# Cross-attention in one core: keys and values by seven block products in place of eight, with a new order of VectorE's work

## The chip, the cores and the metric

The kernel runs on one core of a Trainium2 chip. A core has TensorE (PE in the profile: matrix products, with PEld for the loads of their stationary operand), VectorE (DVE), ScalarE (ACT), GpSimd (POOL) and SyncE (SP, which issues DMAs). Each engine works through its own queue of instructions in order; semaphores tie them together. The products land in PSUM, eight banks of 512 float32 columns on 128 partitions. The metric is the device time of one execution in microseconds (us), lower is better; where several runs are compared it is their median.

## The reference, cut to what matters

All arrays are float32: `x` is 16 x 100 x 640, the context 16 x 722 x 384. The first 718 rows of the context (`enc`) give keys and values; the last 4 (`ca`) go through a second, small attention.

```python
enc, ca = ctx[:, :718], ctx[:, 718:]
hs = mha(x @ Wq, enc @ Wk, enc @ Wv)              # 8 heads of 80, softmax over 718 keys
q1 = einsum('btc,th->bch', ca, Wq_ca)[:, picked]  # 100 of the 384 rows
hs1 = mha(q1, x, x)                               # softmax over 100 keys
hs2 = mha(hs1 @ Wq, ca @ Wk_ca, ca @ Wv_ca)       # softmax over 4 keys
out = (hs + hs2) @ Wout + b_out + x
```

## The kernel before, in words

The 16 batches are worked through one after the other by a Python loop that is unrolled into one program (L743 to L864). In each batch `b`:

- **Scores.** `scores` (L342) multiplies keys by queries for two chunks of key rows at a time. `KC` cuts the 718 rows into five chunks of 128 and one of 78. The result lies in a PSUM tile of four banks (`psum4`, one such tile), from which ACT copies it to `st` (L369), 800 columns (8 heads x 100 queries) for each chunk.
- **Values.** `values` (L247) makes V for a chunk: two halves of 320 columns, each from three products (384 input features are three blocks of 128). The last 78 rows of four batches are taken together: `load_tails` loads them, `last_values` (L278) multiplies them in transposed form once in four batches, and `values` turns them back by transposes (L254). ACT or DVE copies V out of PSUM (L269).
- **Maximum.** DVE takes the maximum of `st` over chunks into `top` (L775, L784, L792), then `over_partitions` (L387) carries it over the partitions: a transpose (L390), a reduction (L392), four copies `side` (L395), four reductions `mx` (L398), a spreading copy (L405), a transpose back (L407). Then it is subtracted from each chunk (L808) and ACT takes the exponential (L810).
- **The second attention** is class `Second`. `products` (L433) makes `y` on PE, `scores1` (L462) makes `e1` on GpSimd, `softmax1` runs the same maximum over `e1` on DVE, `softmax2` (L488) multiplies it by `y` (`z`, L493), takes the softmax over four keys and issues the DMA of `vb` on GpSimd's queue; `values2` (L535) sums on GpSimd. `values2` waits for the last subtraction of L808, and `scores1` and `keys` of later batches follow it in GpSimd's queue.
- **The output.** Class `Last` transposes the result of the batch before (L588), copies it to `hsT` (L597), and `project` (L602) multiplies by `Wout` whenever 128 rows are complete: in all batches but 0, 1, 5, 10 and 14 for the batch before, and DVE adds `x` and bias (L620).
- **Keys of the next batch.** `keys1` (L322): five blocks of 128 columns, two halves of 359 rows, three products each (L329), copied by ACT to `kT` (L336), with the exponentials placed between these copies.
- **Queries** of the next two batches, every second batch (L302).
- **The weighted sum** `a_ps` (L845): 192 products of `st` and V; DVE divides by the sums of the exponentials and adds `hs2` (L853 to L861).

PSUM tiles other than the scores' come from a pool of four single banks (`psum1`): a new tile waits until a bank's last reader is done.

The order on an engine is a planner's, except for GpSimd, which keeps the program's order inside the loop (`manual_schedule`, L742). `issue_after` puts an instruction behind a named one of its own engine. All products are float32, and each shows as two records in the trace.

Of the kernel before, what the change touches and what calls it, by code (L numbers as in the profile page):

```python
# [10 lines left out]
ALU = mybir.AluOpType  # L11
# [10 lines left out]
KC = [(k, min(P, SK - k)) for k in range(0, SK, P)]  # L22
LK, LT = KC[-1]
# [51 lines left out]
VH = [(0, 0, 0, P, 0), (0, 1, 0, P, P), (1, 3, 0, P, 64), (1, 4, 0, P, 192)]  # L75
VH += [(0, 2, 0, 64, 2 * P), (1, 2, 64, P, 0)]
KH = SK // 2
# [3 lines left out]
def kernel(  # L81
# [28 lines left out]
    ps4 = ctx.enter_context(tc.tile_pool(name="ps4", bufs=1, space=PSUM))  # L110
    ps1 = ctx.enter_context(tc.tile_pool(name="ps1", bufs=4, space=PSUM))

    def psum4(name):
        return ps4.tile([P, RG, 512], F32, tag="ps4", name=name)
# [8 lines left out]
    def scores_tile(name):  # L123
        return main.tile([P, ROWS], F32, tag="st", name=name, bufs=len(KC) + 1)
# [21 lines left out]
    def enc_tile(name):  # L146
        return inp.tile([P, CC, SK], F32, tag="enc", name=name)

    def load_enc(b):
        enc = enc_tile(f"enc_{b}")  # L150
        nc.sync.dma_start(out=enc, in_=enct[b])
        return enc

    def load_tails(g):
        tail = inp.tile([P, CC, 4, LT], F32, tag="tail", name=f"tail_{g}", bufs=1)
        for c in range(CC):
            in_order(
                nc.sync.dma_start(
                    out=tail[:, c],
                    in_=enct[4 * g : 4 * g + 4, :, c, LK:].rearrange("b p k -> p b k"),  # L160
                )
            )
        return tail
# [11 lines left out]
    wvca_sb = enc_tile("wvca")[:, :, :H]  # L175
    enc = enc_tile("enc_0")
    for c in range(CC):
        in_order(nc.sync.dma_start(out=enc[:, c, :P], in_=enct[0][:, c, :P]))
        for cols in [slice(0, H // 2), slice(H // 2, H)] if c == 0 else [slice(0, H)]:
            nc.scalar.dma_start(  # L180
                out=wv_sb[:, c, cols], in_=wv[c * P : (c + 1) * P, cols]
            )
    for lo, hi in [(P, 3 * P), (3 * P, SK)]:
        in_order(nc.sync.dma_start(out=enc[:, :, lo:hi], in_=enct[0][:, :, lo:hi]))
# [11 lines left out]
    wq_in = [scores_tile(f"wq_{c}")[:, :H] for c in range(HC)]  # L196
    for c in range(HC):
        in_order(nc.sync.dma_start(out=wq_in[c], in_=wq[c * P : (c + 1) * P]))
    tail = load_tails(0)
# [3 lines left out]

    vs = []
    for k, n in KC:
        v = const.tile([n, NH, D + 1], F32, name=f"v_{k}")
        nc.gpsimd.memset(v[:, :, D : D + 1], 1.0)
        vs.append(v)

# [37 lines left out]
    def values(b, i, enc, engines):  # L247

        k, n = KC[i]
        v_pss = [psum1(f"v_ps_{b}_{i}_{g}") for g in range(2)]  # L250
        if k == LK:

            for g, c, lo, hi, at in VH:
                nc.tensor.transpose(  # L254
                    v_pss[g][:n, at : at + hi - lo],
                    vt[lo:hi, c, (b % 4) * LT : (b % 4 + 1) * LT],
                    ident[lo:hi, lo:hi],
                )
        for g, (engine, v_ps) in enumerate(zip(engines, v_pss)):
            if k != LK:  # L260
                for c in range(CC):
                    nc.tensor.matmul(  # L262
                        v_ps[:n, : 4 * D],
                        enc[:, c, k : k + n],
                        wv_sb[:, c, g * 4 * D : (g + 1) * 4 * D],
                        start=(c == 0),
                        stop=(c == CC - 1),
                    )
            engine(  # L269
                vs[i][:, 4 * g : 4 * g + 4, :D],  # L270
                v_ps[:n, : 4 * D].rearrange("p (h d) -> p h d", d=D),
            )


    def vt_tile(g):
        return inp.tile([P, HC, 4 * LT], F32, tag="vt", name=f"vt_{g}", bufs=1)

    def last_values(g, vt, tail, chunks):  # L278
        for n in chunks:
            t_ps = psum1(f"vt_ps_{g}_{n}")  # L280
            for c in range(CC):
                nc.tensor.matmul(  # L282
                    t_ps[:, : 4 * LT],
                    wv_sb[:, c, n * P : (n + 1) * P],
                    tail[:, c].rearrange("p b k -> p (b k)"),
                    start=(c == 0),
                    stop=(c == CC - 1),
                )
            nc.scalar.copy(vt[:, n], t_ps[:, : 4 * LT])
# [8 lines left out]
    def queries(p, xT, tiles, n):  # L298
# [12 lines left out]
        else:  # L311

            for u in range(2):
                nc.vector.tensor_tensor(  # L314
                    qz[:, 0, :, u * S : (u + 1) * S],
                    q_ps[:, : 2 * S].rearrange("p (j s) -> p j s", j=2),
                    qmask[:, u : u + 1].unsqueeze(2).to_broadcast([P, 2, S]),
                    ALU.mult,
                )


    def keys1(b, enc, chunks, stages=()):  # L322

        stages = list(stages)
        for n in chunks:
            for g in range(2):
                k_ps = psum1(f"kT_ps_{b}_{n}_{g}")
                for c in range(CC):
                    nc.tensor.matmul(  # L329
                        k_ps[:, :KH],  # L330
                        wk_sb[:, c, n * P : (n + 1) * P],
                        enc[:, c, g * KH : (g + 1) * KH],
                        start=(c == 0),
                        stop=(c == CC - 1),
                    )
                copied = nc.scalar.copy(kT[:, n, g * KH : (g + 1) * KH], k_ps[:, :KH])  # L336
                if stages:
                    with tc.issue_after(copied.ins):
                        stages.pop(0)()


    def scores(b, g, tiles):  # L342
# [3 lines left out]
        for a in range(2):  # L346
            k, n = KC[2 * g + a]
            for c in range(HC):
                for r in range(RG):
# [4 lines left out]
                    else:  # L354
                        rhs, lo, hi = qz[rows, 0, b % 2], 0, 2 * S
                    nc.tensor.matmul(  # L356
                        s_ps[:n, r, 256 * a + lo : 256 * a + hi],
# [6 lines left out]
        es = []  # L364
        for a in range(2):
            i = 2 * g + a
            n = KC[i][1]
            e = scores_tile(f"st_{b}_{i}")[:n]
            copied = nc.scalar.copy(  # L369
                e.rearrange("p (r q) -> p r q", r=RG),  # L370
                s_ps[:n, :, 256 * a : 256 * a + 2 * S],
            )
            es.append(e)
        return es, copied
# [12 lines left out]
    def over_partitions(top, name):  # L387

        turned = wide(f"turned_{name}").rearrange("p (b k) -> p b k", k=32)
        nc.vector.transpose(turned.rearrange("p b k -> p (b k)"), top)  # L390
        quad = small.tile([P, NB], F32, tag="quad", name=f"quad_{name}")
        nc.vector.tensor_reduce(quad, turned, AX.X, ALU.max)  # L392
        side = small.tile([32, 4, NB], F32, tag="side", name=f"side_{name}")
        for j in range(4):
            nc.vector.tensor_copy(side[:, j, :], quad[32 * j : 32 * j + 32, :])  # L395
        mx = small.tile([P, NB], F32, tag="mx", name=f"mx_{name}")
        for j in range(4):
            nc.vector.tensor_reduce(  # L398
                mx[32 * j : 32 * j + 32, :],
                side.rearrange("p q b -> p b q"),  # L400
                AX.X,
                ALU.max,
            )
        spread = wide(f"spread_{name}").rearrange("p (b k) -> p b k", k=32)
        nc.vector.tensor_copy(spread, mx.unsqueeze(2).to_broadcast([P, NB, 32]))  # L405
        over = wide(f"over_{name}")
        nc.vector.transpose(over, spread.rearrange("p b k -> p (b k)"))  # L407
        return over
# [13 lines left out]
    class Second:  # L422


        def __init__(self, b, xT):
            self.b, self.xT = b, xT[:, b % 2]

# [5 lines left out]
        def products(self):  # L433
# [14 lines left out]
            nc.vector.tensor_reduce(  # L448
# [4 lines left out]
            )  # L453
            self.y = ys[b % 2]
            self.copied = nc.vector.tensor_copy(
# [24 lines left out]
        def softmax1(self):  # L480
            over = over_partitions(e1, f"1_{self.b}")
            nc.vector.tensor_tensor(e1[:S], e1[:S], over[:S], ALU.subtract)

        def exponentials1(self):
            with tc.issue_after(copied.ins):
                nc.scalar.activation(e1[:S], e1[:S], AF.Exp, scale=SCALE)

        def softmax2(self):  # L488
            b = self.b
            z_ps = psum1(f"z_ps_{b}")  # L490
            for h in range(NH):
# [14 lines left out]
            )  # L506
            s2 = small.tile([S, NH, T], F32, tag="s2", name=f"s2_{b}")
# [12 lines left out]
            nc.scalar.activation(e, e, AF.Exp, scale=SCALE)  # L520
            sm = small.tile([S, NH], F32, tag="sm2", name=f"sm2_{b}")
# [7 lines left out]
            self.vb = vb = vb_tile(f"vb_{b}")  # L529
            nc.gpsimd.dma_start(  # L530
                out=vb[:S],
                in_=va_d[b * T : (b + 1) * T, :].unsqueeze(0).to_broadcast([S, T, H]),
            )
# [27 lines left out]
    class Last:  # L561
# [19 lines left out]
        def transpose(self, chunks=[(0, HC)]):  # L581
# [4 lines left out]
            for c0, c1 in chunks:  # L586
# [4 lines left out]
                for r, (lo, n) in enumerate(OC):  # L591
# [5 lines left out]
                    nc.vector.tensor_copy(  # L597
# [39 lines left out]
    for i in range(len(KC) - 1):  # L637
        values(0, i, enc, (act, dve))
# [14 lines left out]
    room = scores_tile("k2T")  # L653
# [40 lines left out]
    second.products()  # L694
# [3 lines left out]
    with tc.issue_after(second.copied.ins):  # L698
# [13 lines left out]
    keys1(0, enc, range(HC))  # L712
# [29 lines left out]
    ctx.enter_context(tc.manual_schedule(engines={mybir.EngineType.Pool}))  # L742
# [175 lines left out]
```

## Time and profile before

| | |
|---|---|
| median of 3 runs | 1051.35 us (1048.66 to 1051.49) |
| the profiled execution's own time | 1049.26 us |
| its span in the trace | 1047.6 us, granted clock 0.998 |
| matrix records | 11119 |
| start of `a_ps`, batches 0, 7, 8, 10, 15 | 106.3, 553.1, 611.2, 731.6, 1030.6 us |
| a batch, from `a_ps` to `a_ps` | 58.05 us (even), 66.51 (odd, with queries), 74.62 (odd, with queries and tails) |
| DVE busy per batch, mean of batches 1 to 15 | 32.4 us |

The profile is that of one execution. Its page gives busy time by engine, the chain of work that ended last, and groups of instructions by source line. The timeline lists instructions in order of time, with the start and the length of each merged run. A group reads like this: line, engine, operation, what is written from what, shapes, count, busy time in all, mean of one in ns, then the idle time just before and what ended it.

### The profile page before, as it was taken

To read this page: it belongs to the slowest core of one execution; us is meant where nothing else is said; L and a number is where in the kernel's file an instruction comes from. 1 tells how busy PE (TensorE), PEld (TensorE's weight loads), DVE (VectorE), ACT (ScalarE), POOL (GpSimd) and SP (SyncE) were. 2 spreads that over 40 slices of the span, in tenths; PEclk is the share of its full clock that TensorE was granted. 3 is DMA by queue.
4 is the path that set the end of the run, shared out by engine and by line. 5 is a ranking of instruction groups with operands and counts; after the bars stand their busy time and mean duration, and the time that the engine had idled before them with its cause. 6 is when DMAs were issued, how large, how long until landed. Compare 5 with 4: busy or idle time off the path is not lost.

```text
span 1047.6 us, 24702 instructions
## 1 busy us (share of the span) xinstructions
PE 1033.3 (99%) x11119; PEld 774.5 (74%) x11119; DVE 538.6 (51%) x997; ACT 310.2 (30%) x567; POOL 418.9 (40%) x373
## 2 busy tenths in 40 slices
PE   9998999999999999999999999999999999999997
PEld 6784868777687777867778677776868768687775
DVE  1358553828238282565705648064750737528295
ACT  1224231233412334233142332333222233313331
POOL 4629035090720807236180260805445053350833
PEclk9999999999999999999999999999999999999999
DMA  8641011111121111211120211101111021110011
GB/s 280 203 169 46 32 43 47 41 55 40 69 65 34 62 41 43 67 68 47 67 59 27 70 47 63 42 30 43 48 68 46 2 64 48 65 41 1 2 40 33
DMA packets 24347, 61.82 MB, mean 59 GB/s; under 512 B 8462, under 2 KB 14614, under 8 KB 20722
## 3 DMA queue, kind: packets, MB, share of 16 engines
q1 hardware_dynamic: 20994, 42.38, 12.5%
q0 software_dynamic: 2512, 16.72, 4.9%
q8 instruction: 87, 1.43, 0.6%
q10 hardware_dynamic: 736, 1.15, 0.3%
q14 instruction: 18, 0.15, 0.0%
HBM read 55.98 MB, written 4.26 MB: 58 GB/s over the span
## 4 chain that ended last, share of the span: by engine, by line
PE 96%; DVE 3%; DMA 0%; ACT 0%; issue 0%; ACTq 0%; DVEq 0%
PE kT_ps L329 27%; PE v_ps L262 25%; PE s_ps L356 12%; PE a_ps L845 11%; PE q_ps L302 6%; PE o_ps L610 6%; PE vt_ps L282 3%; PE y_ps L439 1%; DVE st L808 1%; PE z_ps L493 1%; PE v_ps L254 1%; PE hst_ps L588 1%; PE m_ps L669 1%; DMA wv_sb<-in_wv 0%; DVE side L395 0%; DVE top L792 0%
## 5 line engine op out<-in xcount | busy, mean ns | idle before, releaser
L544 POOL TENSOR_TENSOR hs<-vb,p 100x640 f32<-100x640 f32 x64 | 84.2, 1324 | 567.9 <-DVE p L525 565.4
L329 PE MATMUL kT_ps<-enc,wk_sb 128*128 128x359 f32 x960 | 296.6, 468 | 6.3 <-ACT kT L336 4.3
L262 PE MATMUL v_ps<-wv_sb,enc 128*128 128x320 f32 x960 | 276.8, 439 | 1.7 <-DVE xn L620 1.1
L329 PEld LDWEIGHTS kT_ps<-enc,wk_sb 128*128 128x128 f32 x960 | 179.9, 190 | 115.4 <-ACT kT L336 5.4
L262 PEld LDWEIGHTS v_ps<-wv_sb,enc 128*128 128x128 f32 x960 | 177.8, 190 | 77.8 <-issue 7.2
L369 ACT COPY st<-s_ps 128x800 f32<-128x800 f32 x96 | 74.5, 828 | 237.4 <-PE s_ps L356 237.4
L269 ACT COPY v<-v_ps 128x320 f32<-128x320 f32 x126 | 53.3, 424 | 209.9 <-PE v_ps L262 202.3
L336 ACT COPY kT<-kT_ps 128x359 f32<-128x359 f32 x160 | 73.1, 458 | 140.8 <-PE kT_ps L329 140.8
L845 PEld LDWEIGHTS a_ps<-v,st 128*36 128x36 f32 (+3 forms) x3072 | 108.9, 125 | 6.5 <-issue 6.3
L845 PE MATMUL a_ps<-v,st 128*36 128x81 f32 (+3 forms) x3072 | 111.9, 233 | 0.5 <-issue 0.5
L314 DVE TENSOR_TENSOR qz<-q_ps,qmask 128x200 f32<-128x200 f32 x16 | 5.1, 361 | 192.5 <-PE q_ps L302 192.5
L356 PE MATMUL s_ps<-qp,kT 32*128 32x100 f32 (+1 forms) x3072 | 102.5, 269 | 0.0
L356 PEld LDWEIGHTS s_ps<-qp,kT 32*128 32x128 f32 (+1 forms) x3072 | 94.1, 179 | 10.2 <-issue 7.3
L469 POOL TENSOR_TENSOR e<-ca,g 100x800 f32<-100x800 f32 x64 | 98.8, 1554 | 5.4 <-DMA ca<-in_cas 2.9
L808 DVE TENSOR_TENSOR st<-st,over 128x800 f32<-128x800 f32 x96 | 100.0, 1076 | 0.4
L853 DVE RECIPROCAL rs<-a_ps 100x4 f32<-100x4 f32 x32 | 5.8, 182 | 183.2 <-PE a_ps L845 183.2
L476 POOL TENSOR_TENSOR e<-e,e 100x800 f32<-100x800 f32 x48 | 91.5, 1906 | 3.8
L810 ACT ACTIVATE st<-st 128x800 f32<-128x800 f32 x96 | 83.6, 872 | 21.3 <-DVE st L808 21.3
L551 POOL TENSOR_TENSOR hs<-hs,hs 100x640 f32<-100x640 f32 x48 | 77.1, 1606 | 3.8
L610 PE MATMUL o_ps<-wout_sb,hsT 128*128 128x320 f32 (+2 forms) x260 | 72.4, 433 | 0.0
L302 PEld LDWEIGHTS q_ps<-xT,wq_sb 128*128 128x128 f32 x400 | 67.9, 190 | 2.1 <-issue 0.5
L302 PE MATMUL q_ps<-xT,wq_sb 128*128 128x200 f32 x400 | 69.1, 333 | 0.0
(81 smaller groups left out, 873.1 us busy)
## 6 DMA issues: line engine op xcount, KB each, us to landing
enc<-in_enct SPq DMA_DIRECT2D x15, 1077.0 KB
vb<-va_d POOLq DMA_DIRECT2D x16, 1000.0 KB, 5.9
xT<-in_xt SPq DMA_DIRECT2D x8, 500.0 KB
xn<-in_x SPq DMA_DIRECT2D x11, 320.0 KB
out<-xn SPq DMA_DIRECT2D x11, 320.0 KB
ca<-in_cas SPq DMA_DIRECT2D x16, 156.2 KB
tail<-in_enct SPq DMA_DIRECT2D x12, 156.0 KB
wout_sb<-in_wqt SPq DMA_DIRECT2D x1, 1600.0 KB
```

What stands on the lines that cost most here:

```text
L262: nc.tensor.matmul(v_ps[:n, : 4 * D], enc[:, c, k : k + n], wv_sb[:, c, g * 4 * D : (g + 1) * 4 * D], start=(c == 0), stop=(c == CC - 1),)
L302: nc.tensor.matmul(q_ps[:, : 2 * S].rearrange("p (j s) -> p j s", j=2), wq_sb[:, c, n * P : (n + 1) * P], xT[:, :, c, :], start=(c == 0), ...
L329: nc.tensor.matmul(k_ps[:, :KH], wk_sb[:, c, n * P : (n + 1) * P], enc[:, c, g * KH : (g + 1) * KH], start=(c == 0), stop=(c == CC - 1),)
L356: nc.tensor.matmul(s_ps[:n, r, 256 * a + lo : 256 * a + hi], kT[rows, c, k : k + n], rhs, start=(a == 0 and c == 0), stop=(c == HC - 1), s ...
L469: first = nc.gpsimd.tensor_tensor(to, self.ca[:, t, :].unsqueeze(1).to_broadcast([S, NH, S]), g[:, :, t].unsqueeze(2).to_broadcast([S, NH, ...
L476: nc.gpsimd.tensor_tensor(e, e, to, ALU.add)
L544: first = nc.gpsimd.tensor_tensor(to, vb[:S, t, :].rearrange("p (h d) -> p h d", h=NH), p2[:, :, t].unsqueeze(2).to_broadcast([S, NH, D]), ...
L551: nc.gpsimd.tensor_tensor(sums, sums, to, ALU.add)
L610: nc.tensor.matmul(o_ps[k][:n, : H // 2], hsTs[r][:, c, :n], wout_sb[:, c, k * (H // 2) : (k + 1) * (H // 2)], start=(c == 0), stop=(c == ...
L808: less = nc.vector.tensor_tensor(st[i], st[i], over[:n], ALU.subtract)
L810: lambda e=st[i]: nc.scalar.activation(e, e, AF.Exp, scale=SCALE)
L845: nc.tensor.matmul(a_v[lo:hi, h % 4], st[i][:, h * S + lo : h * S + hi], vs[i][:, h, :], start=(i == 0), stop=(i == len(KC) - 1),)
```

## The change

The 718 rows are now two halves of 359 (`KH`), each cut into 128, 128 and 103 rows; chunk `i` of the first half and of the second form pair `i`. Two blocks of rows by two blocks of input features by two blocks of columns are multiplied with seven products instead of eight (sums S1 to S4 of `enc` and T1 to T4 of the weights are made ahead, on GpSimd); the third block of features is multiplied as before and added into the same banks, so a pair of V, or two column blocks of K, takes 11 products instead of 12. The tails and their transposes are gone. The fifth column block of K (`last_keys`) keeps six products.

A `Blocks` object does this in two steps: four products into four banks, then seven more on top of them. DVE adds three times after each step, ACT copies once.

```diff
+class Blocks:
+    def first_half(self, room=None):
+        self.banks = room or [psum1(f"{self.name}_ps_{j}") for j in range(4)]
+        c11, c12, c21, c22 = self.to
+        m = self.sum(0, ("11", "11"), first=True)
+        self.copies = [nc.scalar.copy(c22, m)]
+        m = self.sum(1, ("S2", "T2"), first=True)
+        nc.vector.tensor_tensor(c21, m, c22, ALU.add)
+        m = self.sum(2, ("S1", "T1"), first=True)
+        nc.vector.tensor_tensor(c22, m, c22, ALU.add)
+        m = self.sum(3, ("S3", "T3"), first=True)
+        nc.vector.tensor_tensor(c22, m, c22, ALU.add)
+    def second_half(self):
+        c11, c12, c21, c22 = self.to
+        m = self.sum(0, ("12", "21"), ("31", "31"), last=True)
+        self.copies.append(nc.scalar.copy(c11, m))
+        m = self.sum(2, ("S4", "22"), ("31", "32"), last=True)
+        nc.vector.tensor_tensor(c12, m, c21, ALU.add)
+        m = self.sum(3, ("22", "T4"), ("32", "31"), last=True)
+        nc.vector.tensor_tensor(c21, m, c21, ALU.add)
+        m = self.sum(1, ("32", "32"), last=True)
+        nc.vector.tensor_tensor(c22, m, c22, ALU.add)
...
-    ctx.enter_context(tc.manual_schedule(engines={mybir.EngineType.Pool}))
+    engines = {mybir.EngineType.Pool, mybir.EngineType.PE, mybir.EngineType.DVE}
+    ctx.enter_context(tc.manual_schedule(engines=engines))
```

The four-bank tile becomes four tiles of one bank, so ACT copies a pair of score chunks (`st` now holds pairs of 2 x 800 columns) by four copies of 400 columns, one for each bank. The order on PE and DVE is now the program's too. In batches 1 to 13 it is (`va`, `vb`, `vc` are the V pairs, `ka` and `kb` the key blocks; `Maximum` is `over_partitions` in five steps, `go(n)` issues n of them; `side` is now made by reductions):

```python
scores(0); most = max(st[0])          # GpSimd: enc_sums(next enc), last.load()
va.first_half()
scores(1); larger(1)                  # two maxima into most
va.second_half()
scores(2)
now.softmax1(2); last.transpose(); larger(2)
vb.first_half(); now.softmax1(2)
vc.first_half(room)                   # room: the scores' four banks
now.softmax1(); top.go(2)             # rest of e1's maximum and its subtraction
vb.second_half(); now.exponentials1(); top.go(1)
vc.second_half(); top.go()
subtract(0); last.project(); second.products()
now.softmax2(); ka.first_half(room)   # ACT: second.copy()
now.scores2(); subtract(1); now.softmax3()
kb.first_half(); less = subtract(2)
ka.second_half(); kb.second_half(); last_keys()
exponentials                          # GpSimd: values2(less), scores1, keys
queries every second batch; a_ps
```

Batch 0 makes its V by ordinary products, 36 of them, and its maximum follows both first halves of the next keys; the sums of the weights are made in it on GpSimd. In batch 14 the `y` of the last batch comes ahead of `vb`, its `scores1` ahead of `values2`, and its `softmax1` at the end. In batch 15 `softmax2` and `values2` come right after the first scores, and the projection after `vc`. Copies of `hsT` and `y` and the masked copies of `qz` move from DVE to ACT.

## Prediction

> **What bounds the kernel now.** I read the page's busy shares and chain by engine first.
>
> ```profile
> PE 1033.3 (99%) x11119; PEld 774.5 (74%) x11119; DVE 538.6 (51%) x997; ACT 310.2 (30%) x567; POOL 418.9 (40%) x373
> ...
> PE 96%; DVE 3%; DMA 0%; ACT 0%; issue 0%; ACTq 0%; DVEq 0%
> ```
>
> TensorE (PE) is never idle, and 96% of the chain is its own work, so a product less is its pitch less, as long as nothing new makes PE wait. Pitches come from PE's timeline, from a piece's start to the next one's. Batch 8 starts at 560.00 and ends at 618.04.
>
> ```profile
> 576.12 3.42 PE L262 MATMUL v_ps<-wv_sb,enc 128*128 128x320 f32 x12
> 579.38 5.55 PE L610 MATMUL o_ps<-wout_sb,hsT 128*128 128x320 f32 x20
> ...
> 592.10 0.79 PE L254 MATMUL v_ps<-ident,vt 128*78 128x128 f32 x6
> 592.81 18.41 PE L329 MATMUL kT_ps<-enc,wk_sb 128*128 128x359 f32 x60
> 611.15 6.97 PE L845 MATMUL a_ps<-v,st 128*64 128x81 f32 x192
> ```
>
> Each product is two records. A V product takes (579.38-576.12)/6 = 0.543 us (0.541 inside longer runs), a K product 18.34/30 = 0.611 (0.605 without the 0.2 of a start). Next, VectorE (DVE), on which the change puts its additions:
>
> ```profile
> 488.13 1.00 DVE L390 STREAM_TRANSPOSE turned<-e 128x800 f32<-128x800 f32 x1
> 489.17 0.99 DVE L392 TENSOR_REDUCE quad<-turned 128x25 f32<-128x800 f32 x1
> 490.19 0.71 DVE L395 COPY side<-quad 32x25 f32<-32x25 f32 x4
> 490.93 1.32 DVE L398 TENSOR_REDUCE mx<-side 32x25 f32<-32x100 f32 x4
> 492.28 0.99 DVE L405 COPY spread<-mx 128x800 f32<-128x800 f32 x1
> 493.31 1.01 DVE L407 STREAM_TRANSPOSE over<-spread 128x800 f32<-128x800 f32 x1
> 494.35 0.99 DVE L482 TENSOR_TENSOR e<-e,over 100x800 f32<-100x800 f32 x1
> ...
> 502.37 2.07 DVE L792 TENSOR_TENSOR top<-top,st 128x800 f32<-128x800 f32 x2
> ...
> 508.87 0.49 DVE L620 TENSOR_TENSOR xn<-o_ps,xn 128x320 f32<-128x320 f32 x1
> 509.27 0.97 DVE L405 COPY spread<-mx 128x800 f32<-128x800 f32 x1
> ...
> 511.33 2.79 DVE L808 TENSOR_TENSOR st<-st,over 128x800 f32<-128x800 f32 x3
> ```
>
> A maximum with its subtraction is 7.13 us; two `top` steps 2.1; a subtraction's pitch 0.93; an addition out of PSUM (L620) 0.49, pitch 0.40.
>
> **PE's work.** V: before 30 products and 0.71 of transposes a batch, and 15 products (8.33 us) for four batches' tails; after, three pairs of 11. In all, 480 x 0.541 + 60 x 0.555 + 16 x 0.71 = 304.4 against (36 + 15 x 33) x 0.541 = 287.3: -17.1. K: 480 products against 30 + 15 x 28 = 450: -18.2. Scores: 103 rows cost between the 2.67 of two full chunks and the 2.47 of 128 + 78; I take 2.57: +1.6. Together -33.7. An even batch becomes 7.91 scores, 18.31 V, 0.48 transposes, 5.38 projection, 1.06 y, 0.68 z, 17.04 K, 6.89 a_ps = 57.75, the same as batch 8's 58.04: the gain lies in the tails, of which batches 3, 7 and 11 have 8.3 us each, batch 0 8.4.
>
> **What DVE takes on.** A batch gets 30 PSUM additions (18 of 320 columns, 12 of 359); copies of V, y, hsT and qz leave it. That is about 30 x 0.41 - 1.95 - 0.41 - 0.74 - 0.32 = +8.8 on the 32.4 of now: 41 of 58 us. DVE and PE both run in written order, so what counts is the order. A clock from batch start (t = 0):
>
> PE without waits: scores of pair 2 end at 14.2; transposes 14.7; four products of vb 16.95, of vc 19.1, vb's seven 22.9, vc's 26.7; projection 32.1; y 33.15; z 33.8; ka's four 36.3. Then kb's first four need four single banks, and all are held: two by the projection, one by y, one by z, until DVE has read them.
>
> DVE begins at 16.0 (14.2 + 0.14 + four ACT copies of 400 columns: 1.55 for two of 800 bounds them below, 4 x 0.46 of the 359 copy above; I take 1.66). Then: two `most` steps 2.11; vb's additions 0.40 + 0.50 + 0.45 = 1.35 (the third reads the second's result); side, mx, spread 3.06; vc's 1.35; transpose and e subtraction 1.95; `top`'s transpose and reduction 1.99; vb's 1.27; side and mx 2.1; vc's 1.27; spread and transpose 2.06; subtraction of 1600 columns 1.77 (two pitches of 0.93 less one start of 0.09; two durations, 1.96, above): 36.3. The two projection additions end at 36.75 and 37.15, y's sum at 37.35, z at 37.85. So kb starts at 36.75 instead of 36.3: **0.45 us of waiting a batch, 58.2**. Later K steps find their additions done (kb's second at 43.65, needed at 44.7). Everything after t = 16 is one queue; a microsecond more on DVE is one more for PE.
>
> Moves that I cost at nothing: copies of hsT, y and qz go to ACT, which is busy 18 of 58 us; the exponentials (three of 1600 columns, twice 0.87 less a start) follow K's copies and the last subtraction at 46 and end at 48.4, before a_ps at 51.3. If ACT is late with hsT, vb's fourth product waits for its bank, 0.3, in the shadow of kb's wait. The tails' 12 DMAs leave SP's queue; GpSimd issues vb 5.9 us of flight and more before values2. One tile per bank adds no work to PE.
>
> The side reductions have no equal row: four copies 0.71 below, L398's 1.32 above; they resemble the copies (25 columns from 25), so 0.75. Block additions lie between 0.40 and the full 0.49.
>
> **GpSimd.** Its 23 us (values2, scores1, keys; 520.62 to 544.1 in batch 7) wait for the last subtraction, which moves from t = 32 to 46. So after an even batch they run to t = 12 of the odd one, with enc_sums (four of 359 columns; between 0.39 of 128x96 and 1.61 of 100x640, 0.87 by length) and xn to 18. What that costs DVE, batch 0 shows:
>
> ```profile
> 72.95 3.33 DVE L784 TENSOR_TENSOR top<-top,st 128x800 f32<-128x800 f32 x2 [0.85 <-ACT st L369]
> ```
>
> 3.33 instead of 2.1 for two, with GpSimd at work: 1.67 each. Two of L792 in the same batch took 3.75, four of L808 in batch 15 8.09 (2.02 each); 1.03 is the bound below, 2.02 the one above, and I take L784, the same operation. L620 stayed at 0.49 beside GpSimd, so block additions are not slowed. The two steps of pair 1 then end at 12.85 instead of 11.6, the e1 steps at 16.15, pair 2's steps at about 19: DVE is 0.9 late, and part of it is taken up. **Odd batches wait 1.1 us: 67.3** (66.2 with queries). After odd batches GpSimd is done by t = 9: nothing. [...]
>
> enc_sums waits for enc's DMA. It leaves behind the output store, t = 37 of the batch before, and 1.08 MB at the page's 200 to 280 GB/s lands by 43, 15 us early. Behind it queue xn, the vb load and values2, none due before 35.
>
> **Batches without a projection** (1, 5, 10, 14): PE has 5.38 us less, DVE only 0.85 less. kb ends at 37.7 instead of 39.2. In 10, z waits for a vb bank until 29.1, ka's second product for vc's banks until 32.4; the subtraction ends at 36.3, y's sum at 36.5, z at 37.0, and the fourth product of kb follows. So 10 becomes 56.7 (work 52.4; now 53.94); 14, with the next scores1 beside its subtractions, 57.2 (now 53.26); 1 and 5, with 60.8 of work, the 4.3 of batch 10 and 0.3 and 0.8 from GpSimd, 65.4 and 65.9 (now 61.71).
>
> **Ends.** Batch 0 waits for the exponentials. Scores end 5.6 us earlier (6 products in place of 15 and the transposes), block additions give 2.8 back, GpSimd slows the subtractions as now; a_ps starts between 99 (now 106.4) and 105.3, if the last key product waits for a bank and the exponentials behind its copy. I take 101.4: -5. Batch 15: PE 38.1 until a_ps, subtractions done at 35.7, exponentials 37.4; the 4 us of waits at 1024 to 1030 go: 46.6 becomes 45: -1.6.
>
> **Sum.** Five even batches +0.8; five odd ones 356.9 to 336.5: -20.4; 1 and 5 +7.9; 10 and 14 +6.7; ends -6.6. Total -11.6 on the profiled run's own 1049.26 (span 1047.6): 1038. The median of the runs, 1051.35, is 0.2% above that run.
>
> [...]
>
> **Rivals.**
> - *DVE is quicker.* If its queue is 5% shorter (additions overlap more), about 1 us a batch comes back: 0.45 x 5 + 1 x 9 = 11: 1026. For: every pitch here is below its duration. Against: the additions wait for three engines. No waits at all would give about 1010.
> - *DVE decides everything: slower.* Additions cost their full 0.49 because each waits for a semaphore: 12 x 0.09 ahead of kb, and 0.1 at each of six joints: 1.7 a batch, 14 x 1.7 = 24: 1062. It decides from about 1 us a batch. For: a queue with no gap from t = 16 to 48, and GpSimd's overlap could reach further. Against: L620 between other work.
> - *The gain is eaten up exactly*: 0.6 to 1.0 a batch more than worked out, 1046 to 1052. That the products are not saved at all is excluded by their count in the code, 11 for 12.
>
> **Chances.** 0.3%, about what can be told from no change, is 3.2 us: 1046.1 to 1052.4 is the same. Forecast (1031 to 1046) 0.42; quicker DVE 0.24; no change 0.14; slower 0.20. So faster 0.66, same 0.14, slower 0.20. The range goes from half-way past the first rival, 1020, to nearly the second, 1060.
>
> **What would show it.** V records 1062, K 900. Batch 8 near 58.2, 7 near 67.3, 10 near 56.7, a_ps of batch 0 at 101.4. kb's first products waiting for DVE's xn or z; DVE near 650 us busy. Wrong if PE waits elsewhere (for ACT's copies, for enc_sums), if batch 8 is over 59.5, or if contended steps exceed 2 us.

## The result, and the profile after

The changed kernel takes 1057.47 us (median of 5 runs, 1056.67 to 1060.87) where the kernel before takes 1051.35 (5 runs, 1048.66 to 1051.49): 1.0071 times as long, with a 95% interval from 1.0050 to 1.0093. It is slower by 0.7%, more than the 0.3% that can be told from no change. The profiled execution is the median itself; its span is 1055.8 us, 8.2 above that of before. The forecast of 1038 was wrong in sign; the time lies inside the range, between "eaten up exactly" and the slower rival.

The page's busy shares and its chain by engine, and three of its groups:

```profile
PE 1012.4 (96%) x10945; PEld 745.3 (71%) x10945; DVE 711.7 (67%) x1277; ACT 281.3 (27%) x567; POOL 505.1 (48%) x439
...
PE 63%; DVE 27%; issue 6%; ACT 3%; DMA 0%; DVEq 0%; ACTq 0%
...
L941 DVE TENSOR_TENSOR most<-most,st 128x800 f32<-128x800 f32 (+1 forms) x64 | 82.7, 1292 | 46.5 <-ACT st L505 45.4
...
L299 PE MATMUL k_ps<-enc,wk_sb 128*128 128x359 f32 x240 | 85.0, 476 | 10.0 <-DVE xn L787 7.3
L930 DVE TENSOR_TENSOR st<-st,over 128x1600 f32<-128x1600 f32 (+1 forms) x48 | 91.5, 1910 | 0.5
```

TensorE has 174 records fewer, just the 18 of V, 60 of K and 96 of transposes that were counted, and is busy 20.9 us less. The saving is there, but the span is longer: TensorE went from 99% to 96%, and VectorE, which held 3% of the chain, holds 27%. What TensorE waits for, by the view of waits (engine, line, what it waited for, then us in all, how many times, the longest):

```profile
PEld k_ps L299 <- DVE xn L787: 13.0, 10, 1.6
...
PE room L299 <- DVE v L329: 7.6, 4, 1.9
PE k_ps L299 <- DVE xn L787: 7.3, 10, 1.0
...
PE a_ps L1103 <- DVE kT L329: 6.3, 1, 6.3
```

These are banks: kb's first product (`k_ps`) waits for the bank that VectorE's L787 reads last, ka's second (`room`) for one of vc's additions. The third view is the timeline. TensorE in batch 8, around the place where the prediction put the wait (start, length, then in brackets the idle time before):

```profile
591.88 0.87 PE L299 MATMUL room<-enc,wk_sb 128*128 128x359 f32 x2
592.58 1.37 PE L299 MATMUL room<-enc,wk 128*128 128x359 f32 x4
593.79 0.77 PE L299 MATMUL room<-enc,wk_sb 128*128 128x359 f32 x2
595.06 0.87 PE L299 MATMUL k_ps<-enc,wk_sb 128*128 128x359 f32 x2 [0.50 <-DVE xn L787]
```

VectorE in the same batch, whose first score product starts at 558.03:

```profile
573.87 2.02 DVE L941 TENSOR_TENSOR most<-most,st 103x800 f32<-103x800 f32 x2 [0.93 <-ACT st L505]
575.81 0.48 DVE L318 TENSOR_TENSOR v<-v_ps,v 128x320 f32<-128x320 f32 x1
576.39 0.49 DVE L320 TENSOR_TENSOR v<-v_ps,v 128x320 f32<-128x320 f32 x1
576.99 0.49 DVE L322 TENSOR_TENSOR v<-v_ps,v 128x320 f32<-128x320 f32 x1
577.40 0.70 DVE L542 TENSOR_REDUCE side<-quad 32x25 f32<-32x25 f32 x4
...
585.86 0.48 DVE L329 TENSOR_TENSOR v<-v_ps,v 128x320 f32<-128x320 f32 x1
586.44 0.49 DVE L331 TENSOR_TENSOR v<-v_ps,v 128x320 f32<-128x320 f32 x1
586.85 0.48 DVE L333 TENSOR_TENSOR v<-v_ps,v 128x320 f32<-128x320 f32 x1
...
592.77 1.82 DVE L930 TENSOR_TENSOR st<-st,over 128x1600 f32<-128x1600 f32 x1
594.52 0.88 DVE L787 TENSOR_TENSOR xn<-o_ps,xn 128x320 f32<-128x320 f32 x2
```

From 573.87 (t = 15.84) the queue has no gap, as worked out. The three additions of a first half take 575.81 to 577.40, 1.59 us, and those of a second half 1.39: an addition starts 0.40 us after the one before it, but 0.58 to 0.60 where it writes what the one before reads or writes (L320 writes `c22`, which L318 reads; L331 writes `c21`, which L329 reads). kb starts at t = 37.03.

Batch by batch, from the first score product to the next batch's. "Before" and "after" are the profiled executions:

| batch | before | predicted | after | missed by |
|---|---|---|---|---|
| 0 (to its end, from the span's start) | 113.19 | 108.2 | 110.90 | 2.7 |
| 2, 4, 6, 8, 12, each | 58.04 | 58.2 | 58.60 | 0.4, in all 2.0 |
| 3, 7, 11 | 74.61 | 67.3 | 69.79, 68.30, 68.55 | 4.7 |
| 9, 13 | 67.19, 66.51 | 67.3 | 68.30, 68.29 | 2.0 |
| 1, 5 | 61.72, 61.71 | 65.4, 65.9 | 66.00, 67.25 | 2.0 |
| 10, 14 | 53.26 | 56.7, 57.2 | 57.56, 60.25 | 3.9 |
| 15, to the end | 56.64 | 55.0 | 57.58 | 2.5 |

The misses add up to 19.8 us, the distance from the span that was forecast (1036.0) to 1055.8.

### The profile page after: what moved, and what is told of

Same layout as the page of the kernel before. It is cut to its first block, busy times and chain, and to the rows that moved or that the text cites. A ratio compares the mean times of both kernels' runs of the same rounds, so it can differ in the third digit from the quotient of the medians.

```text
span 1055.8 us, 25004 instructions
## 1 busy us (share of the span) xinstructions
PE 1012.4 (96%) x10945; PEld 745.3 (71%) x10945; DVE 711.7 (67%) x1277; ACT 281.3 (27%) x567; POOL 505.1 (48%) x439
## 4 chain that ended last, share of the span: by engine, by line
PE 63%; DVE 27%; issue 6%; ACT 3%; DMA 0%; DVEq 0%; ACTq 0%
PE a_ps L1103 11%; PE s_ps L495 11%; PE k_ps L299 9%; PE v_ps L299 8%; PE room L299 7%; PE kT_ps L437 7%; PE q_ps L412 6%; DVE mx L547 3%; DVE most L941 3%; DVE over L557 3%; ACT st L505 3%; PE v_ps L274 2%; DVE quad L539 2%; DVE turned L537 2%; DVE side L542 2%
## 5 line engine op out<-in xcount | busy, mean ns | idle before, releaser
L299 PE MATMUL v_ps<-wv_sb,enc 128*128 128x320 f32 x480 | 154.7, 444 | 4.3 <-DVE v L320 1.7
L505 ACT COPY st<-s_ps 128x400 f32<-128x400 f32 (+1 forms) x192 | 80.5, 506 | 240.8 <-PE s_ps L495 240.6
L299 PEld LDWEIGHTS v_ps<-wv_sb,enc 128*128 128x128 f32 x480 | 85.8, 190 | 49.1 <-ACT hsT L764 8.5
L1103 PEld LDWEIGHTS a_ps<-v,st 128*64 128x64 f32 (+3 forms) x3072 | 111.1, 126 | 12.6 <-issue 12.5
L1103 PE MATMUL a_ps<-v,st 128*64 128x81 f32 (+3 forms) x3072 | 113.8, 236 | 6.3 <-DVE kT L329 6.3
L941 DVE TENSOR_TENSOR most<-most,st 128x800 f32<-128x800 f32 (+1 forms) x64 | 82.7, 1292 | 46.5 <-ACT st L505 45.4
L299 PE MATMUL k_ps<-enc,wk_sb 128*128 128x359 f32 x240 | 85.0, 476 | 10.0 <-DVE xn L787 7.3
L930 DVE TENSOR_TENSOR st<-st,over 128x1600 f32<-128x1600 f32 (+1 forms) x48 | 91.5, 1910 | 0.5
L299 PE MATMUL room<-enc,wk_sb 128*128 128x359 f32 x240 | 86.2, 482 | 0.0
L412 PEld LDWEIGHTS q_ps<-xT,wq_sb 128*128 128x128 f32 x400 | 67.9, 190 | 2.1 <-issue 0.5
L437 PE MATMUL kT_ps<-enc,wk_sb 128*128 128x359 f32 x210 | 68.7, 465 | 0.5 <-ACT kT L440 0.5
```

The costliest lines, as they stand in the source:

```text
L299: nc.tensor.matmul(bank[: left.shape[1], : right.shape[1]], left, right, start=(first and i == 0), stop=(last and i == len(products) - 1), ...
L412: nc.tensor.matmul(q_ps[:, : 2 * S].rearrange("p (j s) -> p j s", j=2), wq_sb[:, c, n * P : (n + 1) * P], xT[:, :, c, :], start=(c == 0), ...
L437: nc.tensor.matmul(k_ps[:, :KH], w, a, start=(c == 0), stop=(c == CC - 1))
L505: copied = nc.scalar.copy(st[:, :, 2 * r * S : 2 * (r + 1) * S], s_ps[r][:n].rearrange("p (a q) -> p a q", a=2)[:, :, : 2 * S],)
L930: less = nc.vector.tensor_tensor(st[i], st[i], top.over[:n].unsqueeze(1).to_broadcast([n, 2, ROWS]), ALU.subtract,)
L941: nc.vector.tensor_tensor(most[:n], most[:n], st[i][:, u], ALU.max)
```

## The experiments

Theory A: VectorE's queue, in order and without a gap, holds the banks that TensorE needs next; a microsecond on it is one on TensorE. Rival B: a block product itself is dearer on TensorE than an ordinary one. Rival C: not VectorE's own work but GpSimd's overlap with it. Times are of profiled executions unless said; "even", "odd" and "none" (no projection: 1, 5, 10, 14) are batches. Each experiment but e9 is a single execution. Within one, the even batches agree to 0.03 us; the time before the first scores differs between executions, from 60.6 to 63.1 us, so a small change is read from the batches and not from the span.

**e1: the second attention's maximum taken away** (some seven microseconds of VectorE's work a batch).

```diff
-            if not self.top:
-                self.top = Maximum(e1, f"1_{self.b}")
-            self.top.go(n)
-            if self.top.over is not None:
-                nc.vector.tensor_tensor(e1[:S], e1[:S], self.top.over[:S], ALU.subtract)
+            pass
```

> Leaves out the maximum over e1 and its subtraction (the softmax of the second attention is taken without the shift), so VectorE loses 7.1 us a batch, some 5 of them between the last score copies and the projection's additions. Theory A (VectorE's queue holds the PSUM banks that TensorE needs, microsecond for microsecond): the waits of TensorE go; even batches 58.6 to about 57.8, odd 68.3 to 66.3, batches 1 and 5 to about 61.5, batch 10 to 53, batch 14 to 53.5: span 1055.8 to about 1021. Theory B (the block products or their banks cost TensorE more than their pitch): no more than 5 us gained. Theory C (GpSimd's overlap with VectorE is the cause): odd batches gain, even ones and 1, 5, 10 nothing: about 1045.

Span 1023.0, 32.8 less. Even 57.84, odd 66.30, batch 10 52.63. In batches 1 to 13 TensorE waits nowhere over 0.15 us; batch 8 by windows (busy time of PE, PEld, DVE, ACT, POOL, then the granted clock):

```profile
540.37:598.21 57.84, 57.72 (x656) 41.97 (x653) 36.45 (x67) 16.16 (x32) 21.31 (x22) 1.00 0.18 59
```

All block products are still in it, and TensorE's work is the 57.75 of the prediction: B falls. A holds. Batch 14 missed its expectation: it takes 56.32 where 53.5 was expected, with three waits of 1.05 to 1.24 left.

**e2: one reduction of 0.99 us more on VectorE**, ahead of vb's additions in batches 1 to 14.

```diff
+            nc.vector.tensor_reduce(
+                spare, most.rearrange("p (b k) -> p b k", k=32), AX.X, ALU.max
+            )
             vb.first_half()
```

> One more reduction of 800 columns (0.99 us, the duration of the quad reduction in the trace) on VectorE ahead of vb's additions in batches 1 to 14 (the diff names them all but 0 and 15); its result is not used. Theory A: each such batch is 1.0 us longer, 13 to 15 us in all. Theory B: 0 to 3. Theory C: 0 to 5, none of it in even batches.

Span 1066.6, 10.8 more. Even 59.60: 1.00 for 0.99 of work; batch 8:

```profile
563.22:622.84 59.62, 58.24 (x656) 41.82 (x654) 45.23 (x81) 16.27 (x32) 21.23 (x21) 1.00 0.19 59
```

Odd 69.3: 1.0 more, except in batch 3, which became 0.45 shorter. Batch 5 is 1.7 longer, for its granted clock stays at 0.50 for 6.8 us instead of 3.4; batch 14 is 0.4 shorter although it has the reduction too, and the first batch ends 1.1 earlier, mostly because its scores begin earlier: so the sum stays under the 13 expected. The exchange in an even batch is A at its clearest; GpSimd was left as it was.

**e3: GpSimd's sums cut to their first of four terms.**

```diff
-            for t in range(T):
+            for t in range(1):
```

> GpSimd's two sums (scores1 and values2) take one of their four terms, so that GpSimd's block is some 3 us instead of 21.6; the other terms are left out. Theory A: only the maxima and subtractions that overlapped with GpSimd become shorter: odd batches 68.3 to about 67.1 (batch 3 from 69.8), batch 5 to 66, batch 14 to 58, batch 0 about 3 shorter, even batches unchanged at 58.6: span about 1041. Theory C: below 1030, even batches near 57.7. Theory B: no change.

Span 1044.0, 11.8 less. Even 58.60, unchanged; odd 67.06, 1.2 to 2.7 less; batch 14 2.9, batch 0 2.5 less, batch 5 2.5 more where 1.2 less was expected. The trace of batch 5 has two things that the changed kernel's does not: TensorE stands 1.65 us in the middle of its first scores, with no engine named that it waits for, and the granted clock is 0.50 behind that, from 363.0 to 366.5, besides the later stretch that both have. C explains a part of the odd batches and the ends, nothing of the even ones.

**e4: the reads that free banks first.** The first subtraction, 1.82 us that free no bank, goes behind the projection's additions and `z`.

```diff
             if b:
-                subtract(0)
 ...
                 now.softmax2()
+                subtract(0)
                 ka.first_half(room)
```

> Only the order changes: the first subtraction (1.8 us) comes after the projection's additions, y's sum and z on VectorE, so that the four banks that kb needs are read 1.8 us earlier. Theory A: the wait ahead of kb goes: even batches 58.6 to 58.1, odd 68.3 to 67.3, batch 14 some 1.8 less: span about 1046, unless kb's last additions become the next thing waited for. Theory B and C: within 2 us of 1055.8.

Span 1048.8, 7.0 less. Even 57.84, no wait over 0.12 left:

```profile
588.77 0.77 PE L299 MATMUL room<-enc,wk_sb 128*128 128x359 f32 x2
589.38 0.77 PE L299 MATMUL k_ps<-enc,wk_sb 128*128 128x359 f32 x2
```

Nothing was taken off any engine: kb's wait is a matter of what VectorE does first. Odd batches keep 67.97, since they also wait for vb's and vc's additions (0.23 and 0.52). Batch 14 got longer (61.58), and A's 1046 was not reached.

**e5: V by ordinary products** (12 a pair, copied by ACT), K by blocks. The core of the edit:

```diff
-            va, vb, vc = (values(b, i, e_in) for i in range(NP))
+            va, vb, vc = (
+                (Plain if i in (0, 1, 2) else values)(b, i, e_in) for i in range(NP)
+            )
```

> V of batches 1 to 15 by 12 ordinary products a pair, copied by ACT; the keys keep the blocks, order as in the changed kernel. VectorE loses 18 additions a batch (9 us, 6 of them ahead of kb), TensorE gains three products (1.6 us). Theory A: no waits are left but the work grows: even batches 59.4, odd 67.9, 1 and 5 about 62.7, 10 about 54.2, 14 about 58: span about 1044, less than 1055.8 although there are more products. Rival (the keys' blocks are what costs): 1055 to 1080.

Span 1034.0, 21.8 less with more products: even 59.07, odd 67.53, batch 10 53.69, no wait in batches 1 to 13. Three products at 0.541 should have made an even batch 1.62 longer than 57.84, and it is 1.23. Most of the rest shows in TensorE's timeline: the 22 products of vb and vc take 12.25 in e4, since vb's fourth waits for a bank until ACT has copied `hsT`; the 24 ordinary ones run through in 12.95, at 0.540 each. Without that wait the 22 would take 11.90.

**e6: K by ordinary products** (30, in the scores' banks, copied by ACT), V by blocks.

```diff
-                ka.first_half(room)
+                copies = plain_keys(b + 1, 0, enc)
 ...
+            for n in range(1, HC):
+                copies += plain_keys(b + 1, n, enc)
```

> Keys by ordinary products (30 a batch, in the scores' four banks, copied by ACT), V keeps the blocks. VectorE loses 12 additions a batch (6.6 us), all of them behind z, and kb no longer waits for the single banks; TensorE gains two products (1.2 us). Theory A: even batches about 59.1, odd 68.0, the waits of 1, 5, 10 and 14 for vb's and vc's additions stay in part (64, 64.5, 55.5, 59): span about 1045. Rival (V's additions ahead of z do not matter, the keys' do): even batches below 58.

Span 1038.4. Even 59.05, which is 57.84 and two products of 0.605, no wait over 0.12. Odd 67.50 (batch 11 69.01), 1, 5, 10 and 14 63.73, 63.97, 55.27 and 55.63, with the waits for V's additions that were expected to stay. So V's blocks alone make a faster kernel than before, and so do K's (e5): what loses is both together on one VectorE. The edit changes K's banks as well as the additions, and does not tell the two apart.

**e7: block products where VectorE has room.** e4's order, with vc ordinary in odd batches, vb and vc in those without a projection.

```diff
+PLAIN = {b: (1, 2) if b in (1, 5, 10, 14) else (2,) if b % 2 else () for b in range(1, B)}
```

> The order of e4_z_first, and V's blocks only where VectorE has time: vc by ordinary products in odd batches, vb and vc in 1, 5, 10 and 14. Theory A: even batches 57.8 as in e4_z_first, odd 66.9 (one product more, no waits), 1 and 5 about 62.4, 10 about 54, 14 about 59: span about 1030. Rival: the odd batches stay at 68 because GpSimd's overlap comes ahead of all that.

Span 1021.1: even 57.84, odd 66.84, 1 and 5 61.61, batch 10 53.15 and 14 54.05. The expectation was too cautious. One ordinary pair adds 0.54 to e1's 66.30, just a product. Two add only 0.5 to its 61.10 and 52.63, for there vb is ordinary and, as in e5, does not wait: in batch 10, vb and vc take 12.95 for 12.19 and K's blocks 17.10 for 17.34.

**e8: GpSimd's work moved** (on e4): the sums of `enc` behind pair 2's maxima, batch 0's `scores1` behind the subtractions.

```diff
-        larger(2)
+        made = larger(2)
+        if 0 < b < B - 1:
+            enc_sums(enc, made)
 ...
-            second.scores1()
 ...
+            second.scores1(less)
```

> The order of e4_z_first, and GpSimd's work moved out of VectorE's way: enc_sums and xn after pair 2's maxima, in batch 0 scores1 after the subtractions. Theory A: the contended steps that this frees are one of 0.8 us in odd batches and about 3 us of subtraction in batch 0: odd 68.0 to 67.2, batch 0 from 49.5 to 46.5, even batches unchanged: span about 1041. Rival: GpSimd becomes late for the keys, and no gain.

Span 1042.2, 6.6 less than e4. Odd 66.85 to 67.2. Batch 0 is 1.6 shorter than in e4 where 3 was expected. Its three subtractions, 8.48 in the changed kernel, no longer meet GpSimd:

```profile
92.94 5.28 DVE L934 TENSOR_TENSOR st<-st,over 128x1600 f32<-128x1600 f32 x3
```

**e9: e7 and e8, and the last batch's projection begun ahead of its last transposes.**

```diff
-    last.transpose([(2, HC)])
-    last.project()
+    last.project(lambda: last.transpose([(2, HC)]))
```

> e7_mixed and e8_pool_late together, and in the last batch the first four products of each half of the projection ahead of the last transposes. Theory A: batch 0 some 1.6 us shorter as in e8_pool_late, the last 1.5 us of waiting for hs filled, the rest as in e7_mixed (even 57.8, odd 66.8, 1 and 5 61.6): span about 1018. Rival: with GpSimd later, the sums come too late somewhere and the gain of e7_mixed shrinks.

1020.43 us (median of 5, 1019.73 to 1021.71) against 1050.48 before (9 runs): 0.9722, interval 0.9709 to 0.9736, faster than both kernels. Span 1018.3. The page:

```profile
PE 1004.5 (99%) x10973; PEld 748.7 (74%) x10973; DVE 671.0 (66%) x1193; ACT 294.0 (29%) x595; POOL 491.5 (48%) x440
```

VectorE is still busy 66% of the time, and TensorE is back at 99%.

**e10: the dependent additions set apart.** In the second half the addition into `c22` goes between those into `c12` and `c21`, and its product with it; nothing else changes.

```diff
-            m = self.sum(3, ("22", "T4"), ("32", "31"), last=True)
-            nc.vector.tensor_tensor(c21, m, c21, ALU.add)
             m = self.sum(1, ("32", "32"), last=True)
             nc.vector.tensor_tensor(c22, m, c22, ALU.add)
+            m = self.sum(3, ("22", "T4"), ("32", "31"), last=True)
+            nc.vector.tensor_tensor(c21, m, c21, ALU.add)
```

> The changed kernel with one order turned round in each block's second half: the addition to c22 between those to c12 and c21 (and its product likewise), so that no addition directly overwrites what the one before it reads. In the trace of the changed kernel such a pair starts 0.58 us apart, an independent one 0.40. Theory A: 0.36 us less ahead of kb: even batches 58.6 to 58.2, odd 68.3 to 67.9: span about 1051. Rival (the 0.58 is a wait for the product, not for the order): no change.

Span 1049.4, 6.4 less. Even 58.20, the prediction's own figure; odd 67.9. Most batches give 0.4 of that; 3 and 14 give 1.9 and 2.1, batch 5 takes 0.5 more, and a start that took 1.7 longer hides as much. Starts on VectorE are now 0.39 and 0.40 apart:

```profile
583.96 0.48 DVE L329 TENSOR_TENSOR v<-v_ps,v 128x320 f32<-128x320 f32 x1
584.35 0.48 DVE L331 TENSOR_TENSOR v<-v_ps,v 128x320 f32<-128x320 f32 x1
584.75 0.48 DVE L333 TENSOR_TENSOR v<-v_ps,v 128x320 f32<-128x320 f32 x1
```

0.2 for each of two pairs is 0.4 a batch, and 0.4 is what the even batch gives back.

## Why the prediction was wrong

**What bounds the kernel; the products.** Right before the change; after it, TensorE is stopped by VectorE at the places named. The records (1062 of V, 900 of K) and the even batch's work (57.75, measured 57.84) came out. The gross saving was real.

**The failing step is "vb's additions 0.40 + 0.50 + 0.45 = 1.35"**, and the 1.35 and 1.27 that follow it. The timeline has 1.59 and 1.39: 0.72 a batch ahead of kb. Three independent ones would be 1.20; the forecast gave dependence 0.15 in a first half, which has two such pairs, and 0.07 in a second half with one, and each pair costs 0.2. That is more than the whole 0.40 by which an even batch was missed. Smaller terms gave some back (`most` steps 1.94 for 2.11, side reductions 0.70 for 0.75, the start at 15.84 for 16.0), and kb started at 37.03 instead of 36.75. e10 takes 0.4 of this term away, and the even batch is then 58.20. The 1600-column subtraction, another row without an equal, took 1.82 for the forecast's 1.77.

**"0.45 us of waiting"** was also short as a price. kb's product follows the one at 593.79 by 1.27 us where the pitch is 0.605: 0.66, although the view lists 0.50, since a record is 0.16 longer than the pitch; and after the pause its own record is 0.87 for 0.77. Together 0.76, just what the even batch has over the 57.84 of e1 and e4.

**Odd batches**, "wait 1.1 us: 67.3". The work is 66.30 (e1) for the 66.2 taken. The listed waits are 1.48 (0.96 for kb, 0.52 for one of vc's banks), and with 0.26 for each, as above, 2.0: 68.30. Up to pair 2 VectorE was where the forecast had it: its steps make room for the next addition at 508.77, t = 19.04 for "about 19". Behind that point the odd batches have the same additions of 1.59 and 1.39 as the even ones, and the price of two waits. Nor was "part of it taken up": GpSimd's share of the 1.1 was 0.65, and e3, without most of GpSimd's work, is 1.24 shorter (67.06). VectorE's timeline in batch 7:

```profile
499.29 3.47 DVE L941 TENSOR_TENSOR most<-most,st 128x800 f32<-128x800 f32 x2 [2.12 <-ACT st L505]
...
506.00 2.84 DVE L941 TENSOR_TENSOR most<-most,st 103x800 f32<-103x800 f32 x2
```

The mean of the first row, 1.74, is near the 1.67 forecast for each step beside GpSimd, but the steps are not alike. The first took 2.44 and the second 0.99; in the other row they took 1.19 and 1.61. The chain of work, and GpSimd's timeline beside it:

```profile
499.29 2.45 DVE most L941
```

```profile
499.01 1.87 POOL L631 TENSOR_TENSOR e<-e,e 100x800 f32<-100x800 f32 x1
```

GpSimd's addition ran until 500.88, and the step ended 0.85 later: about as if it had waited for that end and then taken its 0.99. Such a step of 2.43 to 2.68 stands in each odd batch from 3 to 13, and each ended about 0.85 after the GpSimd addition beside it. The additions out of PSUM were not slowed: at 508.77, 509.35 and 509.95, beside GpSimd's addition of 2.29 from 507.96, they took 0.48, 0.49 and 0.49. "1.67 each" had divided a merged row by its count.

**Batches without a projection**, "10 becomes 56.7", and 14 57.2. The work (52.4 taken, 52.63 in e1) and the places were right, the price not. TensorE in batch 10:

```profile
713.38 0.74 PE L652 MATMUL z_ps<-y,e 100*32 100x33 f32 x64 [0.66 <-DVE v L329]
714.05 0.87 PE L299 MATMUL room<-enc,wk_sb 128*128 128x359 f32 x2
716.85 2.26 PE L299 MATMUL room<-enc,wk 128*128 128x359 f32 x4 [1.93 <-DVE v L329]
718.91 1.40 PE L299 MATMUL room<-enc,wk_sb 128*128 128x359 f32 x2
720.10 1.09 PE L299 MATMUL k_ps<-enc,wk_sb 128*128 128x359 f32 x2
```

After the wait of 1.93 the same product takes 1.2 us instead of 0.605 (718.91 to 720.10), and by windows the granted clock (third column from the right) falls at the same time:

```profile
700.93:716.53 15.60, 13.28 (x116) 8.75 (x114) 14.68 (x33) 3.10 (x7) 0.00 (x0) 1.00 0.24 81
716.53:720.53 4.00, 3.68 (x7) 2.27 (x8) 3.83 (x6) 0.00 (x0) 0.00 (x0) 0.60 0.24 93
```

A wait was priced by its length alone. Busy time by the missing share of the clock, from windows of 2 us, gives 1.3 to 1.6 lost in each of these four batches. That is not all added. In e10's batch 10 the clock stays at 1.00, but TensorE waits longer for ACT's copy of `y`, 1.82 for the changed kernel's 0.32, and the batch takes 57.17 against 57.56:

```profile
713.96 1.45 PE L299 MATMUL room<-enc,wk 128*128 128x359 f32 x4 [1.73 <-DVE v L329]
...
719.03 0.87 PE L299 MATMUL k_ps<-enc,wk 128*128 128x359 f32 x2 [1.82 <-ACT y L610]
```

In batch 14 it does add up: from the changed kernel to e10 its waits shrink by 0.7, the clock's 1.5 goes, and the batch by 2.1. That batch's own wait for `z`, 2.69, the forecast had not worked out: the subtraction ahead of `z` took 3.01 beside GpSimd where 1.82 is usual.

**Batch 0**, "I take 101.4: -5". `a_ps` started at 101.86, as good as forecast. But the queue ahead of it had been empty for 6.28 us:

```profile
101.86 9.11 PE L1103 MATMUL a_ps<-v,st 128*64 128x81 f32 x192 [6.28 <-DVE kT L329]
```

192 products took 9.11 instead of 6.97, with 0.50 granted until 106. Before, keys ran through the slow stretch (0.50 from 102 to 104); so 2.2 of the 2.7 missed is the clock again. The bank for which it waited was read behind the three subtractions, contended at 8.48.

**The end**, "the 4 us of waits go: -1.6". Batch 15 became 0.9 longer. The listed waits of before are 1.8 us there (1.08 and 0.74), not 4. Up to `a_ps` it is 0.7 shorter, about half of the 1.6; behind it stands a new wait of 1.44, of the last transposes for VectorE's last addition of `hs2` (L1119). In the written order no product lies between them, and the planner had put three of the projection (six records) there. e9, with that restored and the rest, has 56.66.

**The rivals.** "DVE decides everything" was the one that came, at 0.4 (even), 1.3 (odd) and 1.5 (none, on the mean) over the forecast instead of 1.7 a batch, with the dependent addition in place of "0.49 each" as its price: the place, the cause and the sign were its. Its condition, "from about 1 us a batch", held on the mean: 19.8 over 16 is 1.2. "DVE is quicker" leaned on pitches measured between independent instructions, none of them the pitch of dependent additions. Of the signs named, "batch 8 over 59.5" did not come. "Contended steps exceed 2 us" did, in the odd batches above, and so did PE's waits "for ACT's copies": 0.32 to 0.60 for the copy of `y` in batches 1, 5 and 10, 1.24 in 14. VectorE's 711.7 us against 650 comes mostly from work beside GpSimd: with GpSimd's sums cut (e3) it is 665.9, the additions of `hs2` (L1119) 15.7 for 35.5 and L941 66.6 for 82.7. The 650 was itself low: the forecast's own 8.8 a batch in 14 batches on top of 538.6 makes 662.

**What is shown and what stays open.** Shown: the queue (e1, e2, e4), the dependent additions (e10), GpSimd's part (e3, e8). Read off the trace without an experiment of its own: the clock's share. Batch 3 of the changed kernel is an exception by GpSimd: pair 2's steps there took 1.74 and 2.21, beside another addition, and 1.19 and 1.61 in e2. Open: why batch 14 goes against the rest in e2 and e4, and what the written order is worth by itself, since no run has ordinary products throughout in that order, or the blocks in the planner's.

## What to carry to other kernels

Products saved on the busiest engine are worth only what the next engine in the chain can keep up with: block products for V alone or for K alone are worth 9 and 14 us of span, both together lose 8, and a mixture by batch in a better order, with GpSimd's work moved, gains 29. In a written order, let the reads that free banks come before long work that frees none (7.0 us of span in e4), and keep instructions apart that write what the last one read (starts 0.58 us apart for 0.40). Price an idle stretch of TensorE by its length and by the slower clock that can follow it (1.3 to 1.6 us in each batch without a projection here). Before dividing a merged row by its count, look at the single instructions (2.44 and 0.99 under a mean of 1.74).

## What was not expected of the hardware

- Two VectorE additions of 320 columns out of PSUM start 0.39 to 0.40 us apart when independent, 0.58 to 0.60 when the second writes what the first reads or writes; each is recorded as 0.48 to 0.49 in both cases, so the durations do not show it.
- Beside GpSimd, a VectorE maximum of two SBUF tiles of 800 columns took 2.44 us and the next one 0.99: GpSimd's addition beside the first ended 0.85 before it did. The mean hides this.
- A wait of TensorE costs more than the view lists: 0.76 us for a listed 0.50.
- The granted clock fell to 0.50 after short idle stretches: 1.93 us, with another of 0.66 that ended 3.5 us earlier (batch 10), for 3.4 us. After 1.73 with 0.66 it stayed at 1.00 (e10, batch 10), with 1.73 and 1.07 it fell, for 6.8 us (e10, batch 5), and after 1.65 alone it fell too (e3, batch 5), so no single length decides.
